# Graph layer: experts on routed slots, twelve hot node tiles, and batched 0/1 matrices

## The chip, the core and the metric

The kernel runs on one NeuronCore of a Trainium2 chip, in one launch. The metric is the device time of that launch in microseconds (us). TensorE (PE, with PEld for its weight loads), VectorE (DVE), ScalarE (ACT), GpSimd (POOL) and the DMA queue of SyncE (SP) each work through their own list of instructions in order, and wait for each other by semaphores. The lists are fixed when the program is built.

## The reference

There are 6250 nodes of 256 values, in 49 tiles of 128, and 200,000 edges (src, dst). The array dst is sorted and dense at small values: it is drawn as 6250 u², so low nodes are read by many edges.

```python
xn = layernorm(x)
neigh = xn[dst]                                   # one row per edge
w = sigmoid(relu(neigh @ W1 + b1) @ W2 + b2)
num = segment_sum(neigh * w, src); den = segment_sum(w, src)
x = x + where(den > 0, num / den, 0) + head_mixing(xn)   # 8 heads of 32: one 32x32 matrix a head
f = layernorm(x)
p = softmax(relu(f @ rw1 + rb1) @ rw2 + rb2)      # 6 experts
top_w, top_i = top_k(p, 2); g = softmax(top_w)
out_e = relu(relu(f @ w1[e] + b1[e]) @ w2[e] + b2[e]) @ w3[e] + b3[e]
return x + sum(g[i] * out_e[top_i[i]] for i in (0, 1))
```

## The kernel before

**Edges.** A weighted row `w * xn` is the same for all edges that read a node, so each node's row is computed once and stored as three bf16 terms (`y_rows`, 3 x 258 values). The edges lie in three pieces of 65536 and a rest of 3392. Each piece is sorted by src on VectorE (a bitonic sort; `sort`, lines 268 and 269 carry most of it). Two pieces are "cold": for every 128 edges GpSimd gathers the rows by an indirect DMA (L851), VectorE makes a 0/1 matrix `hot` that says which edge belongs to which node (L859), and TensorE adds up three matmuls (L876). One such unit is a cold step. The third piece is "hot": its dst lie in the first six node tiles, so no rows are gathered. `hot_counts` makes two 0/1 matrices for 128 edges, `fr` for the node read (L1022) and `to` for the node that receives (L1020), one tensor_scalar each; their product (L1029) counts the edges from each read node to each receiver. `hot_sums` multiplies the counts `cn` with the rows `yh`, which stay in SBUF (L1048).

**Blocks and groups.** Edges are summed by blocks of two node tiles (25 blocks). Nodes then go through the rest by groups of four tiles (13 groups, the last of 106 rows): `node_terms` (head mixing, L1073), `before_experts` (layernorm, router), and `experts`. The kernel before computes all six experts for every node: two layers of 512-column f32 matmuls (L1201), a third one (L1218), and VectorE adds gate times result (L1227).

**Order.** The order on all engines is written out by the program. An opening sorts the pieces and computes the node rows. Then class `Work` deals out the rest: after each cold step it spends a credit of TensorE time on two lines of work, `to_sums` (node terms, hot counts, hot sums) and `to_experts`. Work that is off both lines (`before_experts`) runs along in a chain by due times. `step` picks the line that has had less time so far; `hot_counts` gives each count matmul 300 ns of that time, though TensorE needs less for it:

```python
            yield BFNS, 300.0            # hot_counts: what TensorE spends, what the line is charged
...
        first = int(self.time[1] < self.time[0])     # Work.step
        for i in (first, 1 - first):
            took = next(lines[i], None)
```

Both kernels end with a check of what their shortcuts assume; if it failed, a slow path would compute everything again.

Of the kernel before, what the change touches and what calls it, by code (L numbers as in the profile page):

```python
# [17 lines left out]
P = 128  # L18
# [8 lines left out]
HB = 8  # L27
GBUF = 22
AHEAD = 10
HELD = 17  # L30
# [8 lines left out]
class Piece:  # L39
# [4 lines left out]

    def __init__(self, name, start, row, used, cap, first, second):
        self.name, self.start, self.row, self.used, self.n = name, start, row, used, row * P
        self.cap, self.first, self.second = cap, first, second
# [3 lines left out]
def kernel(  # L51
# [44 lines left out]

    nc = tc.nc
# [15 lines left out]
    cold = [Piece("a", 65536, 512, P, 23, 12, 9), Piece("c", 131072, 512, P, 23, 12, 9)]  # L113
    hot = Piece("b", 0, 512, P, 23, 23, 0)
    pieces = cold + [hot]
    FEW = 196608
    NFEW = -(-(E - FEW) // P)
    HOT = 6
# [4 lines left out]
    def hot_range(blk, d):  # L123
        per = hot.n * min(BN, N - blk * BN) / N

        def bound(k, sign):
            at = min(1.0, E / hot.n * (P * k / N) ** 0.5) * per
            return at + sign * 5 * at**0.5

        lo = 0 if d == 0 else int(bound(d, -1) // P)  # L130
        hi = -int(-bound(d + 1, 1) // P)
        return max(0, lo), min(hot.cap, hi)
# [19 lines left out]
    lists = {p.name: dram.tile([p.n + p.cap * P], FP, name=f"list_{p.name}") for p in pieces}  # L152
    yh = const.tile([P, HB, TERMS, W], BF, name="yh")
# [27 lines left out]
    def spread(ap, n, name):  # L181

        t = const.tile([P, n], FP, name=name)
        nc.scalar.dma_start(t, bass.AP(tensor=ap.tensor, offset=ap.offset, ap=[[0, P], [1, n]]))
        return t
# [10 lines left out]
    hp1 = ctx.enter_context(tc.tile_pool(name="e_h", bufs=16))  # L196
# [28 lines left out]
    def keys_of(p):  # L225
# [3 lines left out]
        if p is hot:  # L229
# [4 lines left out]
            nc.vector.tensor_scalar(key, s_i, 8, 18, op0=ALU.logical_shift_right, op1=ALU.logical_shift_left)  # L234
# [8 lines left out]
        return k  # L243

# [47 lines left out]
    def turned(p, k, name, back):  # L292

        o = pool_of(p).tile([P, max(p.row, P)], FP, name=f"{name}_{p.name}", bufs=2)
        if p.row < P:
            ps = sq_ps.tile([P, 4 * P], FP, name="turn")
            a, b = (p.row, P) if back else (P, p.row)
            nc.tensor.transpose(ps[:b, :a], k[:a, :b], ident[:a, :a])
            nc.scalar.copy(o[:b, :a], ps[:b, :a])
            return o[:b, :a]  # L300
        for c0 in range(0, p.row, 4 * P):
            ps = sq_ps.tile([P, 4 * P], FP, name="turn")
            for c in range(4):
                nc.tensor.transpose(ps[:, c * P : (c + 1) * P], k[:, c0 + c * P : c0 + (c + 1) * P], ident)
            nc.scalar.copy(o[:, c0 : c0 + 4 * P], ps)
        return o

    def merged(p, k, m):

        t = turned(p, k, "t", False)  # L310
        yield 0, TURN
        g = h = 1 << (m - 1)
        while g:
            o = pool_of(p).tile([P, max(p.row, P)], FP, name=f"t_{p.name}", bufs=2)
            if p.row < P:
                o = o[: p.row, :P]
            if g == h:
                first(t, o, h, last=2 * h == P)
            else:
                step(t, o, g)  # L320
            t, g = o, g // 2
            yield took(p.row // 2 if p.row >= P else P // 2), 0
        k = turned(p, t, "k", True)
        yield 0, TURN
        g = p.row // 2
        while g:
            o = pool_of(p).tile([P, max(p.row, P)], FP, name=f"k_{p.name}", bufs=2)
            o = o[:, : p.row]
            step(k, o, g)
            k, g = o, g // 2  # L330
            yield took(p.row // 2), 0
# [42 lines left out]
    gw1_t = const.tile([P, CB, H], FP, name="gw1_t")  # L374
# [7 lines left out]
    vlw_t = spread(vlw, D, "vlw_t")  # L382
    vlb_t = spread(vlb, D, "vlb_t")
# [48 lines left out]

    rstd_n = nw.tile([P, NTILE], FP, name="rstd_n")
# [20 lines left out]
    one_head = const.tile([P, P], FP, name="one_head")  # L454
    centre = const.tile([P, P], FP, name="centre")
# [170 lines left out]
    worst = const.tile([P, 3], FP, name="worst")  # L626
    most = const.tile([P, 1], I32, name="most")
# [102 lines left out]
    def equal_keys():  # L730

        here, there = (
            hw.tile([P, GT, CB, P], FP, name="xt", bufs=3).rearrange("p t c n -> p (t c n)")[:, : hot.row]
            for _ in range(2)
        )
        nc.sync.dma_start(here, lists["b"][: hot.n].rearrange("(p t) -> p t", p=P))
        nc.sync.dma_start(there, lists["b"][256 : 256 + hot.n].rearrange("(p t) -> p t", p=P))
        starts_of(2)
        nc.vector.tensor_reduce(most, raw["b"][1], axis=AX.X, op=ALU.max)
        nc.vector.tensor_scalar(worst[:, 0:1], most, float(HOT * P) - 0.5, None, op0=ALU.is_gt)  # L740
        yield 1500, 6000
        nc.vector.tensor_tensor(here, here, there, op=ALU.is_equal)
        nc.vector.tensor_reduce(worst[:, 1:2], here, axis=AX.X, op=ALU.max)
        yield 1500, 0
# [6 lines left out]
    line_u = [Line(counts(i)) for i in range(3)]  # L751
    line_a, line_a2, line_b = (Line(sort(p)) for p in pieces)
# [3 lines left out]
    line_e = Line(equal_keys(), before=[line_u[2], line_b, line_h])  # L756
    with tc.manual_schedule(engines=ORDERED):
# [3 lines left out]
        line_u[1].before = line_u[2].before = lines_y  # L761
        line_t.before = line_u[0].before = [line_l]
        first_lines = [line_l, line_d] + lines_y + [line_a, line_u[0], line_t]
        while any(a.open for a in first_lines):
            run(first_lines + [line_q, line_h, line_u[1], line_a2, line_u[2], line_b], clock[0] + 1000.0)
# [15 lines left out]
    def window_keys(wt, name):  # L781
# [4 lines left out]
        keys = wn.tile([P, 2 * max(p.cap for p in pieces)], I32, name="keys")[:, :n]  # L786
# [3 lines left out]
    def cold_window(wt):  # L790

        keys, n = window_keys(wt, "a")
        dsts = wn.tile([P, 2 * cold[0].cap], I32, name="dsts")[:, :n]
        nc.vector.tensor_scalar(dsts, keys, (1 << LOW) - 1, None, op0=ALU.bitwise_and)
        srcs = wn.tile([P, 2 * cold[0].cap], I32, name="srcs")[:, :n]
# [9 lines left out]
    for i, (blk, ps) in enumerate(passes):  # L805
        first_step.append(len(steps_c))
        for half in range(min(SB, NTILE - blk * SB)):
# [5 lines left out]
            steps_c += [(i, half, j, j == todo[0], j == todo[-1]) for j in todo]  # L813

    class Cold:
# [18 lines left out]
        def decode(self, i):  # L834
            self.load(i)
            dsts, srcs = cold_window(self.wt.pop(i))
            loc = wn.tile([P, 2 * cold[0].cap], FP, name="loc")[:, : srcs.shape[1]]
# [3 lines left out]
        def make(self):  # L841
# [7 lines left out]
            if (i, j) not in self.gts:  # L849
# [8 lines left out]
            hot1 = hp1.tile([P, P], BF, name="hot1")  # L858
            nc.vector.tensor_scalar(  # L859
                hot1, count[:, half * P : (half + 1) * P], loc[:, j : j + 1], None, op0=ALU.is_equal  # L860
            )
            self.hot[self.made] = hot1
# [37 lines left out]
    with tc.manual_schedule(engines=ORDERED):  # L900
        cold_edges = Cold(lambda p: p is cold[0] or piece_sorted(p))
        beside = [line_c, line_u[1], line_q, line_h, line_a2, line_u[2], line_b, line_e]
# [20 lines left out]
    eb2_t = column(eb2.rearrange("e h -> (e h)"), NX * CB, "eb2_t")  # L923
    eb3_t = wp.tile([NX, D], FP, name="eb3_t")
# [5 lines left out]
    def expert_loads():  # L930
        for e in range(NX):
            for t, w in zip(ew_t, (ew1, ew2, ew3)):
                nc.sync.dma_start(t[:, e], w[e].rearrange("(c p) h -> p c h", p=P))
                yield 0, 4000

# [14 lines left out]

    nodes, kept = {}, {}
# [8 lines left out]
    beside = [line_w, line_u[1], line_q, line_h, line_a2, line_u[2], line_b, line_e]  # L960
# [12 lines left out]
    ohp = ctx.enter_context(tc.tile_pool(name="o_h", bufs=8))  # L973
# [13 lines left out]
    F32NS, BFNS = 1.67, 112.0  # L987
    hot_wt = {}

    def hot_counts(blk):  # L990

        keys, n = window_keys(hot_wt.pop(blk), "b")
        if blk + 1 < NBLK:
            hot_wt[blk + 1] = window_load(blk + 1, [hot], "b")
        hi = op1.tile([P, n], I32, name="hi")
        nc.vector.tensor_scalar(hi, keys, 18, 31, op0=ALU.logical_shift_right, op1=ALU.bitwise_and)
# [6 lines left out]
        nc.vector.tensor_scalar(rd, keys, 8, 1023, op0=ALU.logical_shift_right, op1=ALU.bitwise_and)  # L1003
        rdl = op1.tile([P, HOT, n], FP, name="rdl")
        nc.vector.tensor_tensor(
            rdl,
            rd[:, None, :].to_broadcast([P, HOT, n]),
            first_d[:, :, None].to_broadcast([P, HOT, n]),
            op=ALU.subtract,
        )  # L1010
        yield 0, 0
        cn = op1.tile([P, HOT, BN], BF, name="cn")
        todo = [(d, j) for d in range(HOT) for j in range(*hot_range(blk, d))]
        made, matrices = {}, []
        for i, (d, j) in enumerate(todo):
            while len(matrices) < min(len(todo), i + 6):
                d1, j1 = todo[len(matrices)]
                if j1 not in made:
                    made[j1] = ohp.tile([P, BN], BF, name="to")
                    nc.vector.tensor_scalar(made[j1], count, loc[:, j1 : j1 + 1], None, op0=ALU.is_equal)  # L1020
                fr = ohp.tile([P, P], BF, name="fr")
                nc.vector.tensor_scalar(fr, count[:, :P], rdl[:, d1, j1 : j1 + 1], None, op0=ALU.is_equal)  # L1022
                matrices.append(fr)
            if i == 0:
                yield 0, 3000.0
            j0, j1 = hot_range(blk, d)
            if j == j0:
                pa = bank_h()[:, :BN]
            nc.tensor.matmul(pa, matrices[i], made[j], start=(j == j0), stop=(j == j1 - 1))  # L1029
            if j == j1 - 1:  # L1030
                nc.scalar.copy(cn[:, d], pa)  # L1031
            yield BFNS, 300.0
        return cn

    def hot_sums(blk, u):
# [6 lines left out]
        for t in tiles:  # L1042
# [3 lines left out]
            for d in range(HOT):  # L1046
# [8 lines left out]
                yield 3 * BFNS, 3 * BFNS  # L1055
# [413 lines left out]
```

## Time and profile before

| | |
|---|---|
| median of 17 runs | 2085.31 us (2081.12 to 2091.55) |
| the profiled execution | 2081.56 us, of which the span of the trace is 2079.4 us |
| granted TensorE clock, mean | 0.923 |
| instructions in the trace | 31214 |
| GpSimd: row gathers (L851) | x1128, 1081.1 us busy, 958 ns of one |
| VectorE: `hot` (L859), `fr` (L1022), `to` (L1020) | x1272, x1105, x562; 271, 269 and 305 ns of one |
| TensorE: cold matmuls (L876), counts (L1029), hot sums (L1048) | x3816, x1105, x882 |
| TensorE: experts (L1201, L1218) | x1248 and x1176 passes (an f32 matmul is two passes) |
| DMA | 311.06 MB, of which 232.33 MB on GpSimd's queue |

Busy time is the time in which an engine worked on at least one instruction. The mean duration of an instruction can be longer than the distance from one start to the next, because instructions of an engine overlap. In the timeline the columns are start, duration of the merged run, instruction, and in brackets how long the engine had been idle and what ended it. A line that ends in "xcount | busy, mean ns | idle" is a group of equal instructions. The first cold gather starts at 243.8 us, the last at 1865.8 us.

### The profile page before, as it was taken

How to read it: one execution, taken by the hardware profiler on the slowest of the kernel's cores; microseconds unless marked ns; L12 is line 12 of the kernel's file. 1: busy time of each engine (PE TensorE's matmuls, PEld its weight loads, DVE VectorE, ACT ScalarE, POOL GpSimd, SP SyncE). 2: the span in 40 equal slices, each digit the busy share in tenths (PEclk: the TensorE clock that was granted, in tenths of full speed). 3: DMA queues.
4: the chain of work that ended last, by engine and by line, in shares of the span. 5: the costliest groups of instructions: out<-in, count | busy, mean ns of one | idle time of the engine just before them, and what ended most of it. 6: DMA issues, size and time to landing. Idle time of an engine off the chain costs nothing.

```text
span 2079.4 us, 31214 instructions
## 1 busy us (share of the span) xinstructions
PE 1798.1 (86%) x10048; PEld 1218.2 (59%) x10048; DVE 1328.0 (64%) x5556; ACT 540.1 (26%) x1100; POOL 1156.2 (56%) x1195
## 2 busy tenths in 40 slices
PE   0664499635588999999999999999999999999998
PEld 0342377423455676666666667666666666766556
DVE  8989778948786655556655556655656566565322
ACT  0675443100011212212121221212122122222332
POOL 0000267877556777676777767677777767760000
PEclk9765599757799999999999999999999999999999
DMA  8842356576546566565665656566565666650000
GB/s 254 232 155 82 88 136 164 122 198 199 151 127 176 149 166 182 148 190 149 180 172 155 188 145 178 162 164 189 159 180 158 164 180 164 195 140 18 1 11 14
DMA packets 158714, 311.06 MB, mean 150 GB/s; under 512 B 28859, under 2 KB 101728, under 8 KB 158544
## 3 DMA queue, kind: packets, MB, share of 16 engines
q0 software_dynamic: 77728, 232.33, 42.4%
q1 hardware_dynamic: 75460, 76.12, 11.8%
q8 instruction: 81, 1.33, 0.3%
q10 hardware_dynamic: 5356, 0.55, 0.2%
q14 instruction: 89, 0.73, 0.1%
HBM read 275.51 MB, written 33.40 MB: 149 GB/s over the span
## 4 chain that ended last, share of the span: by engine, by line
PE 69%; DVE 6%; DMA 1%; issue 1%; ACT 0%; DVEq 0%; SPq 0%; ACTq 0%
PE px L1201 24%; PE pu L876 18%; PE px L1218 12%; PE ph L1029 5%; PE ph L1048 5%; PE px L1188 1%; DVE fr L1022 1%; PE ph L1073 1%; PE px L1108 1%; DVE to L1020 1%; DVE hot L859 1%; PE px L1101 0%; PE px L1114 0%; DVE k_b L268 0%; DVE k_b L269 0%
## 5 line engine op out<-in xcount | busy, mean ns | idle before, releaser
L851 POOL DMA_INDIRECT gt<-y_rows,dsts x1128 | 1081.1, 958 | 677.8 <-DVE srcs L796 241.6
L876 PE MATMUL pu<-gt,hot 128*128 128x258 bf16 x3816 | 627.3, 283 | 3.2 <-DMA gt<-y_rows,dsts 2.6
L876 PEld LDWEIGHTS <-hot 128*128 128x128 bf16 x3816 | 382.3, 101 | 341.5 <-issue 257.8
L1022 DVE TENSOR_SCALAR fr<-count,rdl 128x128 bf16<-128x128 bf16 x1105 | 272.2, 269 | 93.9 <-PE ph L1029 92.5
L1210 ACT ACTIVATE h<-px,eb_t 128x512 f32<-128x512 f32 (+1 forms) x312 | 206.5, 662 | 429.3 <-PE px L1201 428.4
L859 DVE TENSOR_SCALAR hot<-count,loc 128x128 bf16<-128x128 bf16 x1272 | 292.1, 271 | 19.7 <-PE pu L876 18.7
L1201 PE MATMUL px<-fT,ew_t 128*128 128x512 f32 (+1 forms) x624 | 298.2, 573 | 0.3 <-ACT fT L1102 0.3
L1201 PE MATMUL px<-h,ew_t 128*128 128x512 f32 (+1 forms) x624 | 297.1, 570 | 0.0
L1218 PE MATMUL px<-ew_t,h 128*128 128x256 f32 (+1 forms) x1176 | 296.6, 380 | 0.0
L1227 DVE SCALAR_TENSOR_TENSOR acc<-px,gate,acc 128x256 f32<-128x256 f32 (+1 forms) x294 | 128.5, 477 | 196.6 <-PE px L1218 196.4
L1029 PE MATMUL ph<-to,fr 128*128 128x256 bf16 x1105 | 224.9, 279 | 20.1 <-DVE fr L1022 15.0
L1218 PEld LDWEIGHTS px<-ew_t,h 128*128 128x128 f32 (+1 forms) x1176 | 203.3, 190 | 25.0 <-issue 4.3
L1020 DVE TENSOR_SCALAR to<-count,hloc 128x256 bf16<-128x256 bf16 x562 | 170.5, 305 | 2.1 <-PE ph L1029 2.1
L1031 ACT CAST cn<-ph 128x256 bf16<-128x256 f32 x150 | 55.8, 372 | 361.3 <-PE ph L1029 361.3
L1029 PEld LDWEIGHTS <-fr 128*128 128x128 bf16 x1105 | 108.7, 99 | 66.1 <-DVE fr L1022 40.2
L1048 PE MATMUL ph<-yh,cn 128*128 128x258 bf16 x882 | 131.0, 273 | 0.0
L1058 DVE TENSOR_TENSOR cs<-ph,cs 128x258 f32<-128x258 f32 x49 | 20.9, 427 | 151.0 <-PE ph L1048 150.5
L1201 PEld LDWEIGHTS px<-fT,ew_t 128*128 128x128 f32 x624 | 96.3, 191 | 21.9 <-issue 14.9
L1201 PEld LDWEIGHTS px<-h,ew_t 128*128 128x128 f32 x624 | 95.8, 190 | 22.1 <-issue 17.6
L1048 PEld LDWEIGHTS <-cn 128*128 128x128 bf16 x882 | 85.7, 97 | 15.4 <-issue 2.3
L545 PE MATMUL turn<-ident,xs 128*128 128x128 f32 (+1 forms) x98 | 28.2, 407 | 75.2 <-ACT xs L536 72.6
L545 PEld LDWEIGHTS turn<-ident,xs 128*128 128x128 f32 (+1 forms) x98 | 17.0, 195 | 86.8 <-issue 49.5
(238 smaller groups left out, 1718.1 us busy)
## 6 DMA issues: line engine op xcount, KB each, us to landing
gt<-y_rows,dsts POOLq DMA_INDIRECT x1128
xs<-in_x_dram SPq DMA_DIRECT2D x24, 512.0 KB
y_rows<-ys SPq DMA_DIRECT2D x10, 774.0 KB
table<-zero SPq DMA_DIRECT2D x50, 129.0 KB
tb<-table SPq DMA_DIRECT2D x49, 129.0 KB
xnT_d<-xnT SPq DMA_DIRECT2D x12, 512.0 KB
xt<-xnT_d SPq DMA_DIRECT2D x12, 512.0 KB
u<-in_x_dram SPq DMA_DIRECT2D x12, 512.0 KB
```

The costliest lines, as they stand in the source:

```text
L851: nc.gpsimd.indirect_dma_start(out=gt.rearrange("p k w -> p (k w)"), out_offset=None, in_=y_rows, in_offset=bass.IndirectOffsetOnAxis(ap=d ...
L859: nc.vector.tensor_scalar(hot1, count[:, half * P : (half + 1) * P], loc[:, j : j + 1], None, op0=ALU.is_equal)
L876: nc.tensor.matmul(self.pu, hot1, gt[:, k], start=(start and k == 0), stop=(stop and k == TERMS - 1))
L1020: nc.vector.tensor_scalar(made[j1], count, loc[:, j1 : j1 + 1], None, op0=ALU.is_equal)
L1022: nc.vector.tensor_scalar(fr, count[:, :P], rdl[:, d1, j1 : j1 + 1], None, op0=ALU.is_equal)
L1029: nc.tensor.matmul(pa, matrices[i], made[j], start=(j == j0), stop=(j == j1 - 1))
L1031: nc.scalar.copy(cn[:, d], pa)
L1048: nc.tensor.matmul(pu[:, :W], cn[:, d, s * P : (s + 1) * P], yh[:, d, k], start=(d == 0 and k == 0), stop=(d == HOT - 1 and k == TERMS - 1),)
L1201: nc.tensor.matmul(ph[:, :rows], w[:, e, c, f * P : (f + 1) * P], ins[:, c, :rows], start=(c == 0), stop=(c == CB - 1),)
L1210: nc.scalar.activation(h[:, f, :rows], ph[:, :rows], AF.Relu, bias=bc)
L1218: nc.tensor.matmul(po[:r, j - j0], h2[:, c, j * P : j * P + r], ew_t[2][:, e, c, :], start=(c == 0), stop=(c == CB - 1),)
L1227: nc.vector.scalar_tensor_tensor(acc[:r, j, :], po[:r, j - j0], gate[:r, j, e : e + 1], acc[:r, j, :], op0=ALU.mult, op1=ALU.add)
```

## The change

1. **Pieces.** Four pieces instead of three: cold are now `a` (32768 edges) and `c` (65536), hot are `b` (65536) and a new `e` (32768). Hot edges read node tiles 0 to 11 instead of 0 to 5 (`HOT` and `HB` 12). A block has 41 cold steps instead of 52 and 35 gathers instead of 46, and 75 count matmuls instead of 45; hot sums take 12 x 3 matmuls for a tile instead of 6 x 3.
2. **0/1 matrices of four tiles per instruction.** `hot` and `fr` are made up to four at a time and `to` two at a time, by a tensor_tensor of the bf16 count against an f32 operand that is broadcast, instead of a tensor_scalar for each.
3. **Routing.** Groups 0 to 10 form four chunks (three, three, three and two groups). In a chunk each node gets a place among the slots of its two experts (`before_experts` ranks them by small matmuls, `route` turns ranks into rows). GpSimd scatters every node row twice into `slot_rows` in HBM, which was filled with zeros in the opening. `slots` runs the three layers on tiles of 256 slots, each of one expert (17, 17, 17 and 13 tiles); ScalarE reads the expert's number into a register and copies that expert's weights. `combined` gathers the two results of each node and adds them with their weights. Groups 11 and 12 still run all six experts, now by two tiles at a time.
4. **Order and buffers.** `Work.step` no longer weighs the two lines; it asks the sums first. Two chains (routing, combining) run along; a gather or scatter in a chain is spaced by `PACE`, 2500 ns. Buffers: gathered rows 22 to 16, held sums 17 to 13, `cn` 2 to 1, 8 of `to` and `fr` each to 4 (of 2 and 4 matrices).

The diff, cut:

```diff
-HB = 8
-GBUF = 22
+HB = 12
+GBUF = 16
 AHEAD = 10
-HELD = 17
+HELD = 13
@@
-    cold = [Piece("a", 65536, 512, P, 23, 12, 9), Piece("c", 131072, 512, P, 23, 12, 9)]
-    hot = Piece("b", 0, 512, P, 23, 23, 0)
+    cold = [Piece("a", 98304, 256, 12, 7, 4), Piece("c", 131072, 512, 23, 12, 9)]
+    hot = [Piece("b", 0, 512, 23, 23, 0), Piece("e", 65536, 256, 12, 12, 0)]
-    HOT = 6
+    HOT = 12
+    READ = [range(0, 6), range(5, HOT)]
+    CHUNKS = [range(0, 3), range(3, 6), range(6, 9), range(9, NGRP - 2)]
+    DENSE = range(NGRP - 2, NGRP)
@@ class Cold, make
-            hot1 = hp1.tile([P, P], BF, name="hot1")
-            nc.vector.tensor_scalar(
-                hot1, count[:, half * P : (half + 1) * P], loc[:, j : j + 1], None, op0=ALU.is_equal
-            )
+            if a == self.made:
+                k = batch_len[a]
+                self.batch = hp1.tile([P, 4, P], BF, name="hot1")
+                nc.vector.tensor_tensor(
+                    self.batch[:, :k],
+                    count[:, None, half * P : (half + 1) * P].to_broadcast([P, k, P]),
+                    loc[:, j : j + k, None].to_broadcast([P, k, P]),
+                    op=ALU.is_equal,
+                )
@@ hot_counts
-                    made[j1] = ohp.tile([P, BN], BF, name="to")
-                    nc.vector.tensor_scalar(made[j1], count, loc[:, j1 : j1 + 1], None, op0=ALU.is_equal)
-                fr = ohp.tile([P, P], BF, name="fr")
-                nc.vector.tensor_scalar(fr, count[:, :P], rdl[:, d1, j1 : j1 + 1], None, op0=ALU.is_equal)
+                fr = ohp.tile([P, 4, P], BF, name="fr")
+                nc.vector.tensor_tensor(
+                    fr[:, :k],
+                    count[:, None, :P].to_broadcast([P, k, P]),
+                    rdl[:, d1 - READ[i1][0], j1 : j1 + k, None].to_broadcast([P, k, P]),
+                    op=ALU.is_equal,
+                )
+                ...
+                        to = ohp.tile([P, 2, BN], BF, name="to")
+                        nc.vector.tensor_tensor(
+                            to[:, :q],
+                            count[:, None].to_broadcast([P, q, BN]),
+                            loc[:, c0 + j2 : c0 + j2 + q, None].to_broadcast([P, q, BN]),
+                            op=ALU.is_equal,
+                        )
-            yield BFNS, 300.0
+            yield BFNS
@@ route (new), per tile j and expert choice i
+                nc.gpsimd.indirect_dma_start(
+                    out=c.rows,
+                    out_offset=bass.IndirectOffsetOnAxis(ap=c.pos[:, j, i : i + 1], axis=0),
+                    in_=fs[j],
+                    in_offset=None,
+                )
+                yield PACE
@@ slots (new), one round: transposes of tile i, layer 1 of i-1, layer 2 of i-2, layer 3 of i-3
+                nc.scalar.copy(turned_in[i], pT)
+                which[i] = nc.scalar.value_load(c.expert[0:1, i : i + 1], min_val=0, max_val=NX - 1)
+                first_h[a] = yield from layer(own_w.pop((a, 0)), turned_in.pop(a), SLOT, ...)
+            weights(i, 0)
+            ...
+                nc.scalar.copy(own_w[i, k][:, None], ew_t[k][:, bass.ds(which[i], 1)])   # in weights(i, k)
@@ Work.step
-            lines = [self.sums, self.late]
-            first = int(self.time[1] < self.time[0])
-            for i in (first, 1 - first):
-                took = next(lines[i], None)
+            for line in (self.sums, self.late):
+                took = next(line, None)
                 if took is not None:
...
```

## The prediction

> **What bounds the kernel now.** I read the page's first two parts, then stretches, then the order of instructions on each engine around one block of two node tiles. First TensorE's busy time, then busy tenths of TensorE and VectorE and the clock in 40 slices of 52 us:
>
> ```profile
> PE 1798.1 (86%) x10048; PEld 1218.2 (59%) x10048; DVE 1328.0 (64%) x5556; ACT 540.1 (26%) x1100; POOL 1156.2 (56%) x1195
> ...
> PE   0664499635588999999999999999999999999998
> ...
> DVE  8989778948786655556655556655656566565322
> ...
> PEclk9765599757799999999999999999999999999999
> ```
>
> Up to slice 12 VectorE leads (it sorts); behind that TensorE has no gap. Two stretches of the same work, busy us of PE, PEld, DVE, ACT, POOL, then the clock:
>
> ```profile
> 578.00:591.00 13.00, 11.29 (x63) 6.01 (x62) 12.96 (x77) 1.94 (x6) 3.77 (x4) 0.87 0.19 52
> ...
> 1000.00:1200.00 200.00, 199.28 (x1156) 133.51 (x1154) 120.16 (x560) 43.62 (x84) 145.68 (x154) 0.99 0.63 173
> ```
>
> The first is the hot count of one early block, before any expert work exists: VectorE is full (12.96 of 13.00), and the clock falls to 0.87. In the second the hot counts are still there, but expert matmuls lie between them, and TensorE is full. So the count itself is VectorE's; what hides it is expert work in TensorE's order. The timeline shows the rates (start, us, instruction; in brackets the idle time before it):
>
> ```profile
> 571.85 1.16 PE L1048 MATMUL ph<-yh,cn 128*128 128x258 bf16 x9
> 572.86 0.49 PE L876 MATMUL pu<-gt,hot 128*128 128x258 bf16 x3
> ...
> 574.29 0.24 PE L785 MATMUL pT<-ident,wt_b 23*128 23x23 f32 x1
> 577.90 1.76 PE L1029 MATMUL ph<-to,fr 128*128 128x256 bf16 x5 [3.37 <-DVE fr L1022]
> ```
>
> ```profile
> 577.40 0.28 DVE L1020 TENSOR_SCALAR to<-count,hloc 128x256 bf16<-128x256 bf16 x1
> 577.59 0.25 DVE L1022 TENSOR_SCALAR fr<-count,rdl 128x128 bf16<-128x128 bf16 x1
> 577.76 0.28 DVE L1020 TENSOR_SCALAR to<-count,hloc 128x256 bf16<-128x256 bf16 x1
> ```
>
> ```profile
> 183.87 1.23 DVE L590 TENSOR_TENSOR ys<-rest,ys 128x1032 bf16<-128x1032 f32 x1
> 185.02 0.42 DVE L268 TENSOR_TENSOR k_a<-k_a 128x256 f32<-128x256 f32 x1
> 185.35 0.42 DVE L269 TENSOR_TENSOR k_a<-k_a 128x256 f32<-128x256 f32 x1
> ```
>
> ```profile
> 1963.28 3.62 PE L1218 MATMUL px<-ew_t,h 128*128 128x256 f32 x16
> 1966.74 3.60 PE L1201 MATMUL px<-fT,ew_t 128*128 128x512 f32 x8
> ```
>
> ```profile
> 1002.08 0.95 POOL L851 DMA_INDIRECT gt<-y_rows,dsts  x1 [0.30 <-issue]
> 1003.33 0.95 POOL L851 DMA_INDIRECT gt<-y_rows,dsts  x1 [0.30 <-issue]
> ```
>
> Start to start: a bf16 matmul 0.112 us (1.01 for 9), an f32 pass of 256 columns 0.216 (3.46 for 16; a matmul is two passes), `to` 0.19 to 0.20, `fr` 0.165, an indirect DMA 1.25 on GpSimd. A TENSOR_TENSOR holds VectorE 0.33 for 256 elements and 1.15 for 1032: 0.07 + n/960 us.
>
> **The change, part by part.** Counts are from the order of instructions of both kernels.
>
> TensorE, by these rates. Expert matmuls 762 us to 410 (64 slot tiles of 256 rows and five dense tiles for 49 tiles times six experts), 256 transposes of slot rows +27, cold sums 3816 to 3009 matmuls -90, hot counts 1105 to 1863 +84, hot sums 882 to 1764 +99. In all 1632 to 1402: -230.
>
> VectorE, the 0/1 matrices. `fr`: 1105 x 0.165 = 182 becomes 348 of 512 elements at 0.603, 99 of 384 at 0.47, 25 of 256, 124 of 128: 290 us. `to`: 562 x 0.20 = 112 becomes 425 x 0.603 + 25 x 0.34 = 265. Cold `hot`: 1272 x 0.17 = 216 becomes some 155. No row shows a TENSOR_TENSOR with a bf16 and an f32 SBUF operand at 512 elements. The nearest:
>
> ```profile
> L478 DVE TENSOR_TENSOR few_eq<-dv,few_f 128x512 bf16<-128x512 f32 x6 | 4.1, 683 | 0.0
> L482 DVE TENSOR_TENSOR dup<-few_eq,before 128x512 bf16<-128x512 bf16 x6 | 2.5, 425 | 0.2
> L590 DVE TENSOR_TENSOR ys<-rest,ys 128x1032 bf16<-128x1032 f32 x10 | 12.3, 1228 | 2.1 <-ACT ys L588 2.1
> ```
>
> L478 is the same comparison with an f32 operand broadcast (683 ns alone, 0.60 start to start less the overlap of 0.08 that L590 shows), L482 has bf16 alone (425, so 0.345). `loc` and `rdl` stay f32: I take 0.603 and keep 0.345 and 0.683 as ends. So a `to` costs more than before (0.30 for 0.20) and an `fr` barely less (0.151 for 0.165).
> The old form gets 128 more columns for 0.03 us (0.165 to 0.195), the new form pays 0.13 for them. [...]
>
> The order. `Work.step` shared TensorE between sums and experts by time; now it always asks the sums first, and `hot_counts` never yields None. In the order of TensorE a block's hot count then has 75 matmuls (45 before) and about nine cold steps, and no slot matmul. I cut both orders at the first VectorE instruction of each hot list (`hi`) and at its last 0/1 matrix: 25 count stretches and 25 rests. In the count stretches before: TensorE 671 us, VectorE 537. After: TensorE 269, VectorE 643. A typical block: 33 against 25 before, 10.5 against 25.2 after. TensorE waits there in order, with cold steps and slots queued behind it.
>
> Test of the method on the kernel before: the larger of TensorE/0.985, VectorE + 0.8 (transpose and copy of the keys) and 1.25 per indirect DMA in each piece gives 713 + 787 = 1500 us; measured from 553 to 2079.4: 1526. I carry the 26 over as the end's latencies.
>
> The sum after:
> - Opening to the first count: VectorE 411 to 424 us of instructions by these rates (four sorts for three, two of them half as long): 553 + 13 = 566. The 64 zero writes are behind loads on SP: nothing, as DMA share is 0.42 from 100 to 200 us; without that cover, 16.8 MB at the 238 GB/s of the first 100 us, 70.
> - Count stretches: 643 + 25 x 0.8 = 663.
> - Rests: TensorE 950/0.985 = 964; where GpSimd has more (blocks without slots, and block 18 with 75 indirect DMAs), it leads even when it runs nine gathers ahead (16 buffers, six held for both halves): +73, 1037 in all. With no run-ahead 1097.
> - The end: +26.
> - Clock: 0.87 over 13 us is 1.7 us per block; if each spills into the rest, 41; hidden by VectorE's lead, nothing. I take 15.
> Span 566 + 663 + 1037 + 26 + 15 = 2307; 2.2 outside it (2081.6 against 2079.4), and the median lies 3.7 above the profiled run: **2313 us**.
>
> At nothing: 192 weight copies and 128 more copies on ACT (586 ns for 512, the `fT` row) and 64 register loads; ACT was at 26% and gets to some 31%; in the last 11 slot tiles, where TensorE needs 5.6 us each, ACT needs 6 to 7: at most 15. 88 scatters and 88 gathers take GpSimd's turn (counted above at 1.25; the accumulating scatter of before held it 1.93, +60 at most, half of it in rests that GpSimd leads). Each scatter waits for the landing of the one before, with one or two gathers between. A landing on the critical chain took 3.24 us: gone if two gathers lie between, else up to 2 us for each, and cold gathers queue behind it. SP has some 280 more transfers; a late window load would hold the next decode, but SP waited 769 us in all for VectorE's `cs` already and stopped nothing.
>
> **The rivals.**
> Faster or equal: the batched comparison runs at L482's 0.345. Then the stretches are 445 us instead of 663, the clock loss goes too, and the time is 2080, not slower; it decides from there, 0.345 us per 512 elements. Against it: the f32 operand, and L478.
> Faster: TensorE's total decides, slots fill the counts: 2085 - 230 = 1855. For it: TensorE is full from 660 us on. Against it: the order has no slot matmul in a count.
> Slower still: the scatter chain holds GpSimd, 88 x 2 us, and clock and landing losses come on top: 2520. For it: the wait is in the program. Against it: chunks are scattered while VectorE leads for a third of the time.
>
> **How the numbers follow.** VectorE leads the counts: 0.75, its own range 2170 to 2460 (no fixed part per comparison -57, opening hidden -26; 0.683 and no overlap +65, no run-ahead +60). Fast comparison 0.11, half of it just below the old time; TensorE alone 0.06; scatter chain 0.08. The range 2075 to 2460 leaves out the TensorE case, half of the fast comparison and most of the scatter chain. Bound of "no change": 0.2% (4 us), about what a measurement of this kernel can tell. Faster 0.12, same 0.03, slower 0.85.
>
> **What would show it.** After: comparisons of 512 elements near 690 ns; stretches of some 25 us, once per block, with VectorE full, TensorE about 45% busy and a clock below 1; TensorE's waits led by the hot matrices, some 350 us; busy PE down by 200 us in a longer span. Wrong if the comparison takes under 450 ns, if slot matmuls stand inside the counts, or if VectorE's busy share of a block is below 0.6.

## The result, and the profile after

The changed kernel takes 2425.01 us (median of 8 runs, 2419.61 to 2430.53), against 2084.25 us for the kernel before (median of 47 runs): a ratio of 1.163, 95% interval 1.1614 to 1.1646. The forecast was 2313 us, in a range of 2075 to 2460: the direction and the main mechanism held, 112 us of the loss were not in the sum. The profiled execution has a span of 2422.3 us and a mean granted clock of 0.844 (0.923 before).

The page of the changed kernel, the busy times and four rows of its 40 slices, now of 61 us each:

```profile
PE 1781.4 (74%) x10713; PEld 1304.9 (54%) x10713; DVE 1484.6 (61%) x4212; ACT 706.3 (29%) x1652; POOL 1334.5 (55%) x1104
...
PE   1564884456787766889897488888842888888898
...
DVE  8888889677878746555466445665632554446602
...
POOL 0000277667877657665665776666567456477111
PEclk9666895658898877999998689999865999988899
```

The row of nines that TensorE had from slice 13 on is gone, no other engine is full in its place, and the clock drops again and again. Three stretches, cut at the first instruction of a block's hot count (`hi`) and at its last 0/1 matrix, show the three kinds of time that the kernel now has (busy us of PE, PEld, DVE, ACT, POOL, then the clock, DMA share and GB/s):

```profile
1205.02:1230.07 25.05, 17.02 (x96) 9.39 (x96) 24.95 (x55) 4.16 (x12) 15.77 (x7) 0.86 0.26 81
1230.07:1280.18 50.11, 48.48 (x318) 38.67 (x318) 22.89 (x92) 19.64 (x42) 26.78 (x26) 1.00 0.54 152
1305.20:1357.07 51.87, 26.93 (x176) 19.06 (x176) 10.21 (x23) 1.83 (x6) 37.30 (x38) 0.71 0.54 155
```

The first is a hot count: VectorE is busy for 24.95 of 25.05 us, as forecast (25.2). The second is a rest with slot matmuls: TensorE is nearly full, and the stretch is 50.1 us where the rates gave 46.8. The third is a rest in which a chunk's rows are scattered: no engine's busy share is full, TensorE is busy for half, and GpSimd works through 38 instructions, which at 1.25 us from start to start are 47.5 of the 51.87 us. The sum had 26 us for this one.

Inside the hot count the three instructions behave like this (the groups of VectorE with different shapes apart; then TensorE's and GpSimd's timeline):

```profile
L1125 DVE TENSOR_TENSOR to<-count,hloc 128x512 bf16<-128x512 bf16 x425 | 280.3, 683 | 0.0
```

```profile
1207.51 1.19 PE L1137 MATMUL ph<-to,fr 128*128 128x256 bf16 x4 [2.85 <-DVE to L1125]
1209.32 0.98 PE L1137 MATMUL ph<-to,fr 128*128 128x256 bf16 x3 [0.62 <-DVE to L1125]
```

```profile
1206.06 1.01 POOL L887 DMA_INDIRECT gt<-y_rows,dsts  x1 [0.30 <-issue]
1211.21 8.73 POOL L887 DMA_INDIRECT gt<-y_rows,dsts  x1 [4.14 <-PE pu L918]
1220.24 1.48 POOL L887 DMA_INDIRECT gt<-y_rows,dsts  x1 [0.31 <-issue]
```

The comparison takes 683 ns, the matmuls come in small bursts behind it, and a gather that takes 0.95 us elsewhere is on GpSimd for 8.73 us. In the count of the kernel before, with VectorE just as full (578 to 591 us, shown in the prediction), four indirect DMAs took 3.77 us together. Over the whole run the 859 cold gathers take 1222 ns in the mean, for 958 before. That was in no part of the prediction.

By the same cuts the profiled run divides as follows (us). The last row takes the last rest, the end and the sum's 15 us for the clock together with the rests.

| | sum | measured |
|---|---|---|
| opening to the first count | 566 | 565.8 |
| 25 count stretches | 663 | 667.0 |
| rests, end and clock | 1037 + 26 + 15 = 1078 | 1041.7 + 147.7 = 1189.4 |

All of the miss is in the third row, and there in few places: the six rests in or behind which a chunk's rows are scattered are 104 us longer than the sum had them one by one. Each of the others between two counts is within 5 us of it. The trace has 263 indirect DMAs in these six rests, 329 us at 1.25 us each, in 367 us measured; TensorE's work in them is some 191 us by the prediction's rates. So GpSimd leads these rests.

### The profile page after: what moved, and what is told of

Read it like the earlier page. It is cut to its first block, busy times and chain, and to the rows that moved or that the text cites. A ratio compares the mean times of both kernels' runs of the same rounds, so it can differ in the third digit from the quotient of the medians.

```text
span 2422.3 us, 32490 instructions
## 1 busy us (share of the span) xinstructions
PE 1781.4 (74%) x10713; PEld 1304.9 (54%) x10713; DVE 1484.6 (61%) x4212; ACT 706.3 (29%) x1652; POOL 1334.5 (55%) x1104
## 4 chain that ended last, share of the span: by engine, by line
PE 34%; DVE 14%; issue 6%; DMA 4%; POOL 3%; ACT 1%; DVEq 0%; ACTq 0%; SPq 0%; POOLq 0%
PE px L1395 11%; PE pu L918 7%; DVE fr L1114 6%; PE px L1409 5%; DVE to L1125 5%; PE ph L1156 5%; PE ph L1137 2%; DMA got<-slot_made,pos 2%; POOL gt L887 2%; DMA gt<-y_rows,dsts 1%; PE px L1438 1%; PE px L1313 1%; DMA slot_rows<-f_again,pos 1%; POOL slot_rows L1381 1%; DVE hot L898 1%
## 5 line engine op out<-in xcount | busy, mean ns | idle before, releaser
L887 POOL DMA_INDIRECT gt<-y_rows,dsts x859 | 1049.8, 1222 | 778.2 <-DVE srcs L822 276.8
L1137 PE MATMUL ph<-to,fr 128*128 128x256 bf16 x1863 | 393.3, 320 | 239.1 <-DVE to L1125 151.5
L1125 DVE TENSOR_TENSOR to<-count,hloc 128x512 bf16<-128x512 bf16 x450 | 290.7, 668 | 0.0
L898 DVE TENSOR_TENSOR hot<-count,loc 128x512 bf16<-128x512 bf16 (+2 forms) x269 | 170.1, 647 | 141.1 <-PE pu L918 141.1
L1114 DVE TENSOR_TENSOR fr<-count,rdl_b 128x512 bf16<-128x512 bf16 (+2 forms) x323 | 190.8, 612 | 0.0
L1469 POOL DMA_INDIRECT got<-slot_made,pos x88 | 96.5, 1097 | 140.5 <-DMA us<-u_d 56.4
L1381 POOL DMA_INDIRECT slot_rows<-f_again,pos x88 | 110.6, 1256 | 101.6 <-DMA f_again<-f_d 28.0
L1395 PE MATMUL px<-turned_in,w 128*128 128x256 f32 x512 | 137.4, 388 | 3.6 <-ACT w L1428 3.4
L1395 PE MATMUL px<-h,w 128*128 128x256 f32 x512 | 135.0, 381 | 1.0 <-ACT gT L1290 0.9
L1409 PE MATMUL px<-w,h 128*128 128x256 f32 x512 | 130.2, 381 | 4.7 <-ACT w L1428 4.1
L1114 DVE TENSOR_TENSOR fr<-count,rdl_e 128x512 bf16<-128x512 bf16 (+2 forms) x273 | 132.4, 510 | 0.0
L1428 ACT COPY w<-ew_t 128x512 f32 x192 | 118.0, 619 | 1.3 <-DMA gt<-y_rows,dsts 1.0
```

The lines of the kernel that those rows point to most:

```text
L887: nc.gpsimd.indirect_dma_start(out=gt.rearrange("p k w -> p (k w)"), out_offset=None, in_=y_rows, in_offset=bass.IndirectOffsetOnAxis(ap=d ...
L898: nc.vector.tensor_tensor(self.batch[:, :k], count[:, None, half * P : (half + 1) * P].to_broadcast([P, k, P]), loc[:, j : j + k, None].to ...
L1114: nc.vector.tensor_tensor(fr[:, :k], count[:, None, :P].to_broadcast([P, k, P]), rdl[:, d1 - READ[i1][0], j1 : j1 + k, None].to_broadcast( ...
L1125: nc.vector.tensor_tensor(to[:, :q], count[:, None].to_broadcast([P, q, BN]), loc[:, c0 + j2 : c0 + j2 + q, None].to_broadcast([P, q, BN]) ...
L1137: nc.tensor.matmul(pa, reads[a], targets[i, j], start=(a == ends[d][0]), stop=(a == ends[d][1]))
L1381: nc.gpsimd.indirect_dma_start(out=c.rows, out_offset=bass.IndirectOffsetOnAxis(ap=c.pos[:, j, i : i + 1], axis=0), in_=fs[j], in_offset=None,
```

## The experiments

The theories in the expectations, as they were formed along the way: **A**, VectorE's own time in the counts, with nothing else in TensorE's order, is the whole loss. **B**, in addition a comparison with two SBUF inputs holds GpSimd, and the rests pay for gathers that did not run ahead. **C**, the routing's own indirect DMAs, the scatters above all, take GpSimd's turns and hold the gathers up behind them. **D**, TensorE lacks work until a chunk is collected and scattered. **S** and **T** are two readings of C: the standstill before the first scatter of a chunk, or the turns of all 88.

### The comparisons alone

One tensor_scalar for each matrix again, and everything else as changed:

```diff
-                nc.vector.tensor_tensor(fr[:, :k], count[:, None, :P].to_broadcast([P, k, P]), rdl[...].to_broadcast([P, k, P]), op=ALU.is_equal)
+                for q in range(k):
+                    nc.vector.tensor_scalar(fr[:, q], count[:, :P], rdl[:, d1 - READ[i1][0], j1 + q : j1 + q + 1], None, op0=ALU.is_equal)
```

(`to` and `hot` likewise.)

> The changed kernel with all three 0/1 matrices made by one tensor_scalar each again; routing, hot tiles and order stay. VectorE in the count stretches: 75 x 0.165 + 34 x 0.2 + cold ones = 23 us for 25, so 55 us less in all. Theory A (only VectorE's own time counts): 2425 - 55 = 2370 us. Theory B (a comparison with two SBUF inputs also holds GpSimd, so that gathers do not run ahead and the rests between the counts pay some 110 us): gathers back at 0.95 us inside the counts, 2425 - 55 - 110 = 2260 us. Theory C (scatters and combining gathers of the routing are what GpSimd lacks time for): 2370 us, rests as before.

Measured: 2316.36 us, ratio to before 1.1118 (1.1088 to 1.1149), so 109 us less than the changed kernel. The cold gathers among its groups of instructions (count, busy us, mean ns, then GpSimd's idle time before them and what ended it):

```profile
L887 POOL DMA_INDIRECT gt<-y_rows,dsts x859 | 829.4, 966 | 920.5 <-PE pu L916 309.4 <-DVE srcs L822 273.0 <-PE ph L1131 202.4
```

They are back at 966 ns. The counts take 590.1 us, 77 less and not 55: a usual one is 22.0 us, where the expectation had put 23. The rests between the counts shrink by 27 us, not by 110. So both A and B are in it, and neither was sized right: VectorE's part is the larger one, and much of the long rests stays.

### The hold on GpSimd, by itself

Same comparisons on the same tiles, but their `count` operand is read from PSUM. The control only gives up the bank that this needs, the first two lines:

```diff
-    p_x = ctx.enter_context(tc.tile_pool(name="x_ps", bufs=3, space=PSUM))
+    p_x = ctx.enter_context(tc.tile_pool(name="x_ps", bufs=2, space=PSUM))
...
+    count_p = p_c.tile([P, GT * P], FP, name="count_p")[:, :BN]
+    nc.vector.tensor_copy(count_p, count)
...
-                    count[:, None, :P].to_broadcast([P, k, P]),
+                    count_p[:, None, :P].to_broadcast([P, k, P]),
```

> The changed kernel with the same comparisons on the same four or two tiles, but their count operand is read from PSUM (as f32, in one of the three banks of px), so that each has one SBUF input only. VectorE's time for one stays near 0.60 us or grows by at most 0.06. Theory A and C: no gain, 2425 to 2500 us. Theory B: gathers inside the counts at 0.95 us again, the five or six rests that GpSimd leads shrink by 110 us together: 2315 us, up to 2385 if the operand in PSUM is dearer.

> Control for the run with the operand in PSUM: the changed kernel with two banks of px instead of three, nothing else. All theories: 2425 to 2450 us, gathers inside the counts as long as in the changed kernel (8 to 20 us).

Measured: 2421.75 us with the operand in PSUM (1.1615, 1.1589 to 1.164), 2461.14 us for the control (1.1791, 1.1758 to 1.1823), on one chip. The groups with the operand in PSUM:

```profile
L1131 DVE TENSOR_TENSOR to<-count_p,hloc 128x512 bf16<-128x512 f32 x425 | 278.0, 677 | 0.0
```

```profile
L889 POOL DMA_INDIRECT gt<-y_rows,dsts x859 | 826.3, 962 | 1000.2 <-PE pu L920 435.7 <-DVE srcs L822 273.3 <-PE ph L1143 157.8
```

and the gathers of the control:

```profile
L887 POOL DMA_INDIRECT gt<-y_rows,dsts x859 | 1044.6, 1216 | 812.1 <-PE pu L918 293.7 <-DVE srcs L822 275.8 <-issue 133.6
```

VectorE's comparison is as long as before (677 ns), and the long gathers are gone. So it is not VectorE being full that holds GpSimd: with this comparison's second input out of SBUF the hold is gone, and the two runs are 39 us apart, both with two banks. (The operand in PSUM is also f32 where it was bf16.) In the two profiled runs, 46.9 us apart, 32 us of it lie in the six rests around the scatters and 11 in the counts. That B's hold exists and costs time is shown; its price was 110 in the expectation. The bank alone cost 36 us against the changed kernel, which the control was expected to show at 25 at most: without it the run with PSUM would have been read as "no effect".

Two SBUF inputs alone are not enough for the hold, though. In the opening of the changed kernel the sort runs such instructions one behind the other, and the gathers beside them keep their time:

```profile
393.52 0.43 DVE L287 TENSOR_TENSOR k_b<-k_b 128x256 f32<-128x256 f32 x1
393.87 0.41 DVE L288 TENSOR_TENSOR k_b<-k_b 128x256 f32<-128x256 f32 x1
```

```profile
393.49 0.95 POOL L887 DMA_INDIRECT gt<-y_rows,dsts  x1 [0.30 <-issue]
```

There are 46 gathers with these two lines on VectorE for over three quarters of the 2 us around them: 1.02 us in the mean, 1.31 at most. The sort's instructions are shorter (256 elements), f32 and not broadcast; which of these decides was not varied.

### Sixteen-bit operands

```diff
-        loc = op1.tile([P, n], FP, name="hloc")
+        loc = op1.tile([P, n], BF, name="hloc")
```

(`rdl` and the cold `loc` likewise.)

> The changed kernel with hloc, rdl and loc in bf16 instead of f32, so that a comparison has 16-bit operands alone; they hold whole numbers, and what is rounded stays outside the compared range. If a comparison then takes 0.345 us like the 16-bit row of the kernel before: counts 445 us for 667, time 2200 us (theory A and C), or with GpSimd still held as both inputs stay in SBUF about the same less some hold, 2160 to 2200 (theory B). If the broadcast operand keeps it at 0.60: 2425 us.

Measured: 2421.02 us (1.1615, 1.1587 to 1.1644), no change. The group:

```profile
L1125 DVE TENSOR_TENSOR to<-count,hloc 128x512 bf16<-128x512 bf16 x425 | 280.3, 682 | 0.0
```

The prediction's rival "fast comparison" leaned on L482 of the kernel before (425 ns, all operands bf16), and held only the f32 operand against it. That was not the whole reason: with bf16 alone it is still 682 ns. L482 has a broadcast operand too, but one that repeats a whole row of 128 values, where `hloc` and `rdl` repeat a single value along the row; and L482 multiplies, where this compares. Which of these makes the difference is not shown: no run here varied the step alone, or the operation alone.

### The order, alone and with the comparisons

```diff
-            for line in (self.sums, self.late):
-                took = next(line, None)
+            lines = [self.sums, self.late]
+            first = int(self.time[1] < self.time[0])
+            for i in (first, 1 - first):
+                took = next(lines[i], None)
...
+                        self.time[i] += took * 0.8 if i else (300.0 * (took > 0) if isinstance(took, Count) else took)
```

> The changed kernel with the weighing of the two lines by time put back into Work.step (a count charged 300 ns, expert time at 0.8), so that slot matmuls stand between count matmuls again; the batched comparisons stay. Theory A (VectorE's counts with TensorE idle, because of the order): TensorE work in the counts goes from 269 to 527 us by the order of instructions, the larger engine's sums give 799 + 767 us for counts and rests, with opening and end 2160 us, and 2210 to 2260 with the hold and the routing waits still paid. Theory of the scatters alone (C): the rests around the scatters stay as they are and the counts too, 2400 us or more. If VectorE's own work is the limit whatever the order: 2425 us.

> The changed kernel with both: the weighing put back and all 0/1 matrices by tensor_scalar; routing, four pieces and twelve hot tiles stay. A and B: 761 + 761 us for counts and rests by the order, 2110 us with opening and end; with the routing's own waits on GpSimd still there (some 60 to 100 us in five rests) 2170 to 2210 us, just above the kernel before. C (scatters and gathers of the routing cost what is left): not below 2170.

Measured: 2363.36 us for the order alone (1.1314, 1.1272 to 1.1355) and 2278.76 us for both (1.0907, 1.0868 to 1.0946). The order gives 62 us with the batched comparisons and 38 with single ones, the comparisons 85 where the order is weighed and 109 where it isn't. Both expectations were 70 to 150 us too low, and C's bound for the order alone (2400 or more) was too high. Two counts of the run with both:

```profile
884.45:907.06 22.61, 16.86 (x99) 10.24 (x99) 22.49 (x129) 4.18 (x12) 16.06 (x18) 0.81 0.53 154
967.11:1011.71 44.60, 42.48 (x290) 34.43 (x291) 28.13 (x155) 22.35 (x51) 26.77 (x29) 1.00 0.68 201
```

Where slots exist (second line) they fill the count as in the kernel before: TensorE 42.48 of 44.60 us at full clock. Where none exists (first line) VectorE leads again. The weighing can only put in what is there: in this run the rows of the slots are read in four bunches, one for each chunk, with stretches of no slot work between them.

### The batches alone, and the routing alone

The batched comparisons in the kernel before; and the changed kernel with the pieces, six hot tiles, comparisons and weighing of the kernel before:

```diff
-    cold = [Piece("a", 98304, 256, 12, 7, 4), Piece("c", 131072, 512, 23, 12, 9)]
-    hot = [Piece("b", 0, 512, 23, 23, 0), Piece("e", 65536, 256, 12, 12, 0)]
+    cold = [Piece("a", 65536, 512, 23, 12, 9), Piece("c", 131072, 512, 23, 12, 9)]
+    hot = [Piece("b", 0, 512, 23, 23, 0)]
...
-    HOT = 12
-    READ = [range(0, 6), range(5, HOT)]
+    HOT = 6
+    READ = [range(0, HOT)]
```

> The kernel before with the batched comparisons alone (hot and fr four at a time, to two at a time; 21 buffers of gathered rows for 22). VectorE by the rows: to 562 x 0.2 = 112 us becomes 281 x 0.6 = 169, the others about as before, and TensorE has expert matmuls in the counts. Theory A: +15 to +25 us, 2100 to 2110 us. Theory B (the hold on GpSimd, which was at 94% of its maximum): gathers of several us inside the counts, and TensorE waits for gathers: 2130 to 2250 us.

> The routing alone: the pieces, the six hot tiles, the tensor_scalar comparisons and the weighing of the kernel before, with routed slots (16 buffers of gathered rows). TensorE loses 762 - 410 - 27 = 325 us of work. A: GpSimd decides, with 1128 gathers, 88 scatters and 88 combining gathers: 1173 after the opening x 1.25 = 1466, + 553 + the last slots (some 100) = 2120 us. C: the scatters hold the gathers behind them up and it is 2200 us or more. If TensorE's total decides: 2085 - 325 = 1760 us.

Measured: batches alone 2101.17 us (1.0071, 1.005 to 1.0092), as A had it. The gathers are long here too (1045 ns in the mean, 12.2 us at most), but TensorE has expert work in its order, which by A covers most of VectorE's longer counts and of GpSimd's delay. In the changed kernel, with 75 count matmuls a block for 45, the batches cost 85 to 109 us.

Routing alone: 2307.63 us (1.1075, 1.1022 to 1.1129), 223 us slower than before, though it takes 325 us of work from TensorE. The stretch from its first count to the end of its last one, and a piece inside it (columns as above):

```profile
554.63:2187.77 1633.14, 1264.01 (x7840) 937.47 (x7841) 801.74 (x4049) 413.27 (x919) 1113.38 (x1162) 0.84 0.64 184
```

```profile
850.00:900.00 50.00, 19.14 (x75) 10.29 (x74) 4.44 (x23) 0.37 (x1) 34.43 (x37) 0.53 0.45 132
```

GpSimd has 1162 indirect DMAs in 1633 us; at a turn of 1.25 us that is 1452, 89% of the stretch. In the second line TensorE is busy for 19 of 50 us beside 37 of them. Before, the stretch of 200 us shown in the prediction had 154 of them, 96% of GpSimd's rate, so that there was little room for 176 more (220 us at 1.25). The expectation had put the same turns into a sum, 2120 us, as if GpSimd were never idle; C's bound of 2200 held. The twelve hot tiles take 269 gathers away, yet the run above with order and comparisons undone, which differs from this one only in the pieces and the hot tiles, is only 29 us faster: its counts are 779.0 us for 518.1 here, its rests between them 792.1 for 1115.1.

### Chunks and scatters

Six chunks for four, on the run with weighing and single comparisons; and the changed kernel without its scatters and the loads of their rows:

```diff
-    CHUNKS = [range(0, 3), range(3, 6), range(6, 9), range(9, NGRP - 2)]
+    CHUNKS = [range(0, 1), range(1, 3), range(3, 5), range(5, 7), range(7, 9), range(9, 11)]
```

```diff
-                nc.gpsimd.indirect_dma_start(out=c.rows, ...)
-                yield PACE
```

> The run with weighing and tensor_scalar (2279 us), its groups 0 to 10 cut into six chunks (one group, then five of two) for four of three and two; 74 slot tiles instead of 64, so 10 x 5.6 = 56 us more TensorE work. Theory D (TensorE idles while a chunk is collected and scattered, because no slot exists then; the first slots came at 930 us): first slots near 730 us, TensorE filled through the scatters of the next chunk, 2130 to 2200 us. Theory C (GpSimd's turns in the scatter runs set the pace whatever TensorE has to do): 2280 to 2335 us.

> The changed kernel without the 88 scatters of node rows and the loads before them: the slots read the zeros that the opening wrote, so routed experts compute on zero rows, everything else stays. If the runs of scatters are what makes the rests longer than the sum (111 us over): the sum's own price for them (27 us, where GpSimd leads) and most of the 111 go, 2290 to 2320 us. If their price is only GpSimd's turns as in the sum: 2395 us. If they cost nothing because GpSimd was at 55%: 2425 us.

Measured: six chunks 2297.66 us (1.102, 1.0997 to 1.1043), 19 us more than four. The first slots did come at 727 us instead of 929, and D's 2130 to 2200 us did not come: slots that begin 200 us earlier did not bring what D gave for them. A small gain can be hidden in the 19 us, since ten more slot tiles are 56 us of work for TensorE by the expectation.

Without scatters 2293.00 us (1.0994, 1.0971 to 1.1018): 132 us less than the changed kernel, 1.5 us for each scatter. The first slot rows are read at 864.7 us here, 959.7 in the changed kernel, and the slots compute on zeros; neither was separated from the scatters themselves. The rest behind the same count as the one of 51.87 us above:

```profile
1287.21:1341.70 54.49, 42.92 (x284) 34.75 (x284) 17.83 (x42) 17.97 (x40) 42.18 (x41) 0.94 0.72 210
```

It is about as long, but 284 matmuls are in it instead of 176, at a clock of 0.94 for 0.71: the slots come earlier and lie beside the gathers. The three rests around it take 138.7 us with 831 matmuls, in the changed kernel 162.5 with 825. Summed for this kernel's own order, the working of the prediction gives 1010 + 26 + 15 = 1051 us for rests, end and clock; measured 913.6 + 154.0 = 1067.6. So without the scatters the sum holds to 17 us, although the hold on GpSimd is still there (7 indirect DMAs are busy for 16.40 us in one of its counts, 15.77 in the count shown above). Whether the hold costs less without scatters was not tested.

### What in a scatter costs

In the changed kernel the first scatter of a chunk stands at the head of GpSimd's queue until its node row and its places are there:

```profile
1270.39 0.95 POOL L887 DMA_INDIRECT gt<-y_rows,dsts  x1 [0.30 <-issue]
1285.15 9.96 POOL L1381 DMA_INDIRECT slot_rows<-f_again,pos  x1 [13.81 <-DVE to L1125]
```

GpSimd is idle for 13.81 us with gathers behind it, and then held for 9.96 in a count. The four chunks lose 11.3, 13.8, 12.5 and 16.6 us so. The last two runs begin the scatters 25 us of planned time later, on the changed kernel and on the one with weighing and single comparisons:

```diff
         load(0)
         load(1)
+        yield 25000
         for j in range(c.n):
```

> The changed kernel with the scatters of each chunk begun 25 us of planned time later: the first two node rows are loaded as before, then 11 to 20 gathers stand ahead of the first scatter on GpSimd instead of none. Theory S (the first scatter of each chunk waits for its node row and for VectorE's places, 11.3, 13.8, 12.5 and 16.6 us in the trace, with all gathers behind it): 54 us less, 2370 us. Theory T (the price of the scatters is their 88 turns and landings, the standstill is covered): 2425 us, or up to 2450 as the slots come later.

> The run with weighing and tensor_scalar (2279 us) with the same later start of the scatters. Theory S: up to 54 us less, 2225 us. Theory T: 2279 us, or up to 2305 as the slots come later. Either way above the kernel before, unless the later scatters also let TensorE work through them: then below 2200.

Measured: 2405.12 us (1.1534, 1.151 to 1.1559) and 2262.43 us (1.0851, 1.0827 to 1.0876), 20 and 16 us less. The same scatter now follows at once:

```profile
1304.57 0.94 POOL L887 DMA_INDIRECT gt<-y_rows,dsts  x1 [0.31 <-issue]
1305.81 0.99 POOL L1382 DMA_INDIRECT slot_rows<-f_again,pos  x1 [0.30 <-issue]
```

The standstill is gone and gives 20 of its 54 us; whether node row or places ended it was not separated. So S is the smaller part. For the rest of the 132 us T is the reading that is left, not one with a run of its own: 88 turns are 110 us at 1.25, in stretches where GpSimd gives every second or third turn to a scatter, the cold steps wait for the gathers between, and TensorE has nothing else in its order. The last run is the fastest form of the change that was tried. It is still 8.5% slower than the kernel before, which no version here beats.

## Why the prediction was right, and where it was off

- **Comparison.** Sized at 0.603 us from start to start, and near 690 ns for one, where L478 has 683 ns. Measured 683 ns, and 0.60 us from one start to the next in a count (1283.11 to 1283.71 us). The row of the f32 operand (L478) was the right neighbour, though one of its inputs (`dv`) lies in PSUM, but the f32 operand was not needed for it: with bf16 alone it is 682 ns.
- **Count stretches.** 663 us forecast, 667 measured; VectorE full, once per block, the clock at 0.86; TensorE is busy for 17.02 of 25.05 us there, 68%, where the sign was 45%. That the order leaves TensorE idle there is confirmed by undoing it (62 us), and that VectorE's length sets them by undoing the comparisons (77 of 109 us).
- **Opening and slots.** 566 against 565.8; the 64 zero writes and ScalarE's weight copies cost little (TensorE's waits for the copies are under 10 us), and rests with slots run near TensorE's rate (busy for 48.48 of 50.11 us in the one shown).
- **Rests: the step that failed.** "It leads even when it runs nine gathers ahead: +73, 1037 in all", and scatters "counted above at 1.25". The run-ahead does not happen. With the indirect DMAs counted where the trace has them, the larger of TensorE's work by the rates over 0.985 and 1.25 us for each, summed over the rests and the end, is 1100 us: the prediction's own bound, "no run-ahead 1097". That bound was the right one and still too low, since it had no standstill. The sum let scatters cost 27 us net (1037 against 1010 without them); the kernel without them is 132 us faster. Two reasons for the lost run-ahead have a price: the comparisons that fill the counts hold GpSimd in them (39 us), and each chunk's first scatter stops GpSimd's queue (20 us). They are not all: with single comparisons, where the gathers are back at 966 ns, the six rests still have 256 indirect DMAs for 263 and take 348 us for 367. What else keeps the gathers back is open. The smaller numbers of buffers (22 to 16 for gathered rows, 17 to 13 for held sums) were not varied.
- **The scatter rival** (2520 us, 0.08) named the right resource with the wrong wait. It priced 88 landings at 2 us; waits for a scatter's landing are 25.4 us in the trace.
- **TensorE's total** (1855 us) and the **fast comparison** (2080 us) did not occur.
- **Busy PE down by 200 us**, named as a sign, was wrong: 1798.1 to 1781.4. The work by the rates did shrink, but the mean matmul is longer, which fits matmuls that come in small bursts and under a lower clock (0.844 for 0.923): a count matmul 320 ns for 279, a cold one 304 for 283. TensorE's waits are led by the hot matrices, as forecast, but are 225 us, not 350 (its waits: us in total, times, longest):

```profile
PE ph L1137 <- DVE to L1125: 151.5, 155, 8.0
PE pu L918 <- DMA gt<-y_rows,dsts: 112.8, 49, 10.2
PE ph L1137 <- DVE fr L1114: 73.7, 173, 3.8
```

The middle line, waits for gathers, was 2.6 us before for the same matmul: this is the part that the forecast did not have.

The loss of 341 us divides, by the runs, into 109 for the comparisons, 38 more for the order, and 194 that stay with both undone. These 194 are the routing's: alone it costs 223 us, and the twelve hot tiles, put to it in the same order and with the same comparisons, give 29 back. Later scatters give 16 of the 194. How the others split between GpSimd's turns, the chunks and the fewer buffers is open, and no run has the hot tiles without the routing.

## What to carry to other kernels

Work taken from the fullest engine is only worth time if the order still has something to put beside the next engine; here 230 us less TensorE work made the kernel slower, since much of what was left waits for VectorE and GpSimd in order. Count an added indirect DMA as a full turn of GpSimd (1.25 us here) in the stretch where it stands, and look at what is queued behind the first one of a series. When a control is needed for a changed resource (a bank here), run it: it moved the time by 36 us, nearly as much as the effect (39).

## What the runs showed of the hardware

While VectorE ran comparisons of 512 elements with both inputs in SBUF and broadcast, one behind the other (0.60 us from start to start), one indirect DMA stayed on GpSimd for up to 23.2 us (958 ns in the mean of the kernel before). With one input in PSUM (962 ns in the mean) or as tensor_scalar (966 ns) this was gone, though VectorE had as much to do: with one input in PSUM it was busy for 1478.1 us of the run, for 1484.6 in the changed kernel, and with tensor_scalar for 21.90 of 22.00 us of a count. Beside the sort's f32 tensor_tensor of 256 elements, both inputs in SBUF, a gather took 1.02 us in the mean, so two inputs in SBUF did not make the hold by themselves here. What else it takes was not shown. An operand in PSUM did not make the comparison dearer (677 ns for 683).
